# Attention scores from float32r halves in a perceiver layer: queries and keys split in two, the shift in its own product, maxima two heads at a time

## The chip, the core and the metric

The kernel runs on one core of one Trainium2 chip. The metric is the device time of one execution in microseconds, as the median of several executions. The core has five engines that work side by side and wait for each other by semaphores: TensorE (PE, matrix products into PSUM; its weight loads are listed apart as PEld), VectorE (DVE), ScalarE (ACT), GpSimd (POOL) and SyncE (SP, which here only starts DMAs). PSUM has 8 banks of 512 float32 columns on each of 128 partitions.

## The reference

One layer in float32: cross-attention from 256 queries to 4,096 keys, then a causal linear attention, then a gated feed-forward network, each behind a layer normalisation and added to x. B = 4, 16 heads of 16. The change touches the scores of the first part alone:

```python
def xattn(query, key, value):                   # query (4, 256, 256), key = value (4, 4096, 256)
    Q = query @ Wq.T + bq                       # reshaped to 16 heads of 16; K and V alike
    K = key @ Wk.T + bk
    V = value @ Wv.T + bv
    dot = einsum('bhsd,bhtd->bhst', Q, K) / sqrt(16)
    out = einsum('bhst,bhtd->bhsd', softmax(dot, axis=-1), V)
    return out @ Wh.T + bh
x = x + xattn(layernorm(x), ctx, ctx)
```

## The kernel before

**Units and steps.** A unit u is one batch with four heads; there are 16. Each head has 32 partitions of its own, of which 16 hold its dimensions, one holds the shift and the rest are zero. So a product over one head uses a quarter of PE's rows, and four heads can run at once. A unit has 16 steps (NS) of 256 keys; n counts all 256 steps.

**Two passes over the scores.** The softmax subtracts each query's exact maximum, so scores are computed twice. `maxima` (L796) makes them with 128 queries on PSUM's partitions and 512 keys on its columns (pm, L810), one bank a head, and DVE takes the maximum over the columns (mx, L817). `shift` (L821) turns the 16 maxima of a unit's queries into the negated maximum, and POOL's DMAs write it into the free row of a copy of the queries (qa, L830 and L832). As the keys have ones in that row, `scores` (L846) gets shifted scores from one product (pt, L856, keys on the partitions, 256 queries on the columns), and ACT takes the exponential of 512 columns at once (e0 to e3, L861). `product` (L866) multiplies with the values (pav, L876), where a column of ones adds the softmax's sum, and DVE adds to av (L886).

**A step's order.** The order on PE, ACT, DVE and SP is the one in which the program is written. In step n stand: scores of heads 0 and 1 together with maxima of heads 2 and 3 of the step 19 further on (LEAD = 3), then the other way round (L1122 to L1129); one half of an item that makes keys (pk, then ku on ACT) or values (pv, then v); pieces of the causal part from step 180 on (products among them from step 214); pav of step n-1. From step 237 on there are no maxima left.

**Keys.** `key` (L736) makes 512 keys for eight heads, ACT adds the bias into ku (L753), and eight DMAs on SP spread 16 rows each to kt (L756). Three kt buffers of 4,096 columns rotate over the units. They are filled with ones once, before. Queries come the same way: `project` for the first heads, `spread` for the others, with eight POOL DMAs each (L983). `finish` (L888) sends av through DRAM with twelve POOL DMAs a unit; `layernorm` and `queries` make the queries' input.

**The opening** computes all keys of the first pair of units and 19 rounds of maxima with nothing else to wait for (L1085 to L1098). After the last step, the rest of the causal part and the feed-forward network run.

**PSUM.** `bank` (L209) hands out one of eight equal banks; a new tile waits until what was last in its bank has been read.

Of the kernel before, what the change touches and what calls it, by code (L numbers as in the profile page):

```python
# [12 lines left out]
F32 = mybir.dt.float32  # L13
I32 = mybir.dt.int32
AF = mybir.ActivationFunctionType
# [5 lines left out]
P = 128  # L21
# [18 lines left out]
def perceiver_layer(  # L40
# [27 lines left out]
    wq_sb = const.tile([P, KC, NQ * P], F32, tag="wq_sb", name="wq_sb")  # L68
    bq_sb = const.tile([P, NQ], F32, tag="bq_sb", name="bq_sb")

    bk_sb, bqu_sb = (const.tile([P, KC], F32, tag=name, name=name) for name in ("bk_sb", "bqu_sb"))

    def load_queries():
# [7 lines left out]
        nc.scalar.dma_start(out=wq_sb, in_=wqP)  # L81
        nc.scalar.dma_start(out=bq_sb, in_=bqP)

# [110 lines left out]
    qT = qkT = keep.tile([P, NQ, B * T], F32, tag="qT", name="qT")  # L194
    kts = [keep.tile([P, S], F32, tag=f"kt{i}", name="kt") for i in range(3)]
    qk = [kts[1][:, t * 2 * D : (t + 1) * 2 * D] for t in range(NT)]
# [10 lines left out]
    psum = ctx.enter_context(tc.tile_pool(name="psum", bufs=8, space=PSUM))  # L207

    def bank(shape, name):  # L209

        return psum.tile(shape, F32, tag="b", name=name)
# [3 lines left out]
    def causal_in(b, norm_late=None):  # L215
# [21 lines left out]
        def queries_keys(i):  # L237
            t, zT = tiles[i], got[0]
            ps = bank([P, 2 * D], "pqk")
            for k in range(KC):  # L240
                product4(
                    ps, zT[:, k, i * P : (i + 1) * P], rest[3][:, k, : 2 * D],
                    start=k == 0, stop=k == KC - 1,
                )
            nc.vector.tensor_tensor(qk[t], ps, rest[4][:, : 2 * D], ALU.add)
            sqs[i] = lnp.tile([P, 2 * D], F32, tag="sq", name="sq")
# [42 lines left out]
    def qk_turned(t):  # L289
# [3 lines left out]
        (nc.scalar.copy if t >= NT - 2 else nc.vector.tensor_copy)(qkT[:, :, t * P : (t + 1) * P], ps)  # L293

    def feature(n, part):
        i = 2 * (n % 4) + part
        return kts[2 if n % 8 < 4 else 0][:, i * 2 * T : (i + 1) * 2 * T]

    def features(n):

        b, q = divmod(n, NQ)
        cs = slice(b * T, (b + 1) * T)
        pfs = [bank([P, 2, T], "pf") for _ in range(4)]
        for s in range(2):
            for i, pf in enumerate(pfs):
                rows = slice(32 * i, 32 * i + 32)
                nc.tensor.matmul(  # L309
                    pf[:, s, :], lhsT=rest[5][rows, q // 2, :], rhs=qkT[rows, 2 * s + q // 2, cs],  # L310
# [133 lines left out]
    def start_causal():  # L444
# [91 lines left out]
        tc, xr, load_x, load_queries, load_rest, ctxT, wq_sb, bq_sb, bqu_sb, wkP, bk_sb, wvP, eps, ident, layernorm, product4,  # L536
        qT, kts, lnp, dram, bank, rest, start_causal, wff, place, masks)
# [4 lines left out]
    masks(late.tile([P, 3, P], F32, tag="mask", name="mask"))  # L542
    att = late.tile([P, NT, D], F32, tag="att", name="att")
# [683 lines left out]
```

## Time and profile before

| what | us |
|---|---|
| median of 3 runs | 1184.56 (1184.26 to 1185.65) |
| span of the profiled execution, first to last instruction | 1182.7 |
| opening, to the first pt | 74.3 |
| steps 0 to 236 | 930.8 |
| steps 237 to 255 | about 58 |
| after the last pav | about 119 |
| PE, DVE, ACT, POOL busy | 1171.0, 904.8, 696.5, 236.8 |
| exponentials on ACT, 1,024 of them | 529.3 |
| reduces on DVE, 1,024 of them | 634.9 |

The profile was taken in an execution of its own, of which the span is known. A busy share is the time with at least one instruction running; the ends of products on PE are modelled, so a full PE is not PE at its peak. In a group's row stand line, engine, operation, what it writes and reads, shapes, the number of instructions, busy time and mean length, and the idle time before them with what ended it. In the chain, each step is what released the next, from the last instruction back. The f32 products appear twice as often as the program has them.

### The profile page before, as it was taken

The page shows a single profiled execution, that of the slowest core. Times are in us where ns is not written, and L with a number is a line of the kernel's source. Part 1 is how long each engine was busy: PE and PEld are TensorE (multiplying, and loading weights), DVE is VectorE, ACT ScalarE, POOL GpSimd, SP SyncE. Part 2 cuts the span into 40 slices and gives each one's busy share as a digit, 9 for nine tenths or more (in the row PEclk, how much of TensorE's full clock was granted, in tenths as well). Part 3 has the DMA queues.
Part 4 walks back from the last instruction along what each step waited for, and adds up shares of the span by engine and source line. Part 5 has one row for each costly group of instructions (what it writes and reads, how often), then busy time and mean ns, then how long its engine had stood idle before and what let it go on. Part 6 is the DMA issues. An engine that isn't in the chain of part 4 may idle for free.

```text
span 1182.7 us, 42980 instructions
## 1 busy us (share of the span) xinstructions
PE 1171.0 (99%) x18024; PEld 798.5 (68%) x18024; DVE 904.8 (77%) x1723; ACT 696.5 (59%) x1444; POOL 236.8 (20%) x443
## 2 busy tenths in 40 slices
PE   8999999999999999999999999999999999999998
PEld 4476667766776677667766776667666666667777
DVE  7987787777777777877777877798887788567753
ACT  4456666666666655666666665666664456876442
POOL 3730302011111212120202020303031132213210
PEclk8999999999999999999999999999999999999999
DMA  6562442234223432333224322432233112000000
GB/s 211 145 208 66 115 121 81 61 103 114 85 78 87 118 96 74 81 111 101 83 76 117 93 80 75 113 113 83 66 105 111 39 42 69 11 2 10 10 11 18
DMA packets 55160, 99.99 MB, mean 85 GB/s; under 512 B 23392, under 2 KB 28056, under 8 KB 54968
## 3 DMA queue, kind: packets, MB, share of 16 engines
q1 hardware_dynamic: 44904, 91.84, 26.2%
q0 software_dynamic: 9440, 4.81, 2.1%
q8 instruction: 143, 2.34, 0.8%
q10 hardware_dynamic: 624, 0.59, 0.2%
q14 instruction: 49, 0.40, 0.1%
HBM read 76.13 MB, written 3.21 MB: 67 GB/s over the span
## 4 chain that ended last, share of the span: by engine, by line
PE 97%; DVE 2%; ACT 1%; issue 0%; POOL 0%; ACTq 0%; POOLq 0%
PE pt L856 23%; PE pm L810 19%; PE pav L876 19%; PE pv L188 11%; PE pk L188 11%; PE pg L582 2%; PE pd L598 2%; PE pu L582 2%; PE pa L335 1%; PE pqk L188 1%; PE po L361 1%; DVE mx L817 1%; PE py L409 1%; PE pf L309 1%; PE py L188 1%; PE pa L340 1%
## 5 line engine op out<-in xcount | busy, mean ns | idle before, releaser
L861 ACT ACTIVATE e<-pt 128x512 f32<-128x512 f32 x1024 | 529.3, 602 | 374.4 <-PE pm L810 356.6
L817 DVE TENSOR_REDUCE mx<-pm 128x1 f32<-128x512 f32 x1024 | 634.9, 683 | 127.0 <-PE pm L810 126.7
L856 PE MATMUL pt<-qa,kt 32*128 32x256 f32 x4096 | 501.4, 388 | 0.7 <-DVE qa L842 0.5
L810 PE MATMUL pm<-kt,qT 32*128 32x512 f32 x2048 | 498.4, 617 | 0.1
L856 PEld LDWEIGHTS pt<-qa,kt 32*128 32x128 f32 x4096 | 318.0, 184 | 124.0 <-ACT v L781 42.4
L876 PE MATMUL pav<-e,v 128*32 128x256 f32 x4096 | 269.1, 380 | 0.0
L810 PEld LDWEIGHTS pm<-kt,qT 32*128 32x128 f32 x2048 | 181.3, 191 | 15.7 <-DVE mx L817 4.9
L876 PEld LDWEIGHTS pav<-e,v 128*32 128x32 f32 x4096 | 128.5, 110 | 74.0 <-issue 4.6
L886 DVE TENSOR_TENSOR av<-pav,av 128x256 f32<-128x256 f32 x240 | 101.6, 423 | 57.8 <-PE pav L876 57.3
L188 PE MATMUL pv<-wv_sb,wff 128*32 128x128 f32 x4096 | 137.3, 276 | 0.0
L188 PE MATMUL pk<-wff,wk_sb 128*32 128x256 f32 x2048 | 137.1, 389 | 0.0
L188 PEld LDWEIGHTS pv<-wv_sb,wff 128*32 128x32 f32 x4096 | 104.3, 109 | 43.1 <-DVE mx L817 43.1
L188 PEld LDWEIGHTS pk<-wff,wk_sb 128*32 128x32 f32 x2048 | 54.7, 110 | 66.6 <-DVE mx L817 38.8
L925 POOL TENSOR_TENSOR oT<-oT,bvT 128x64 f32<-128x64 f32 x32 | 8.6, 290 | 357.8 <-DVE oT L922 356.2
L908 POOL DMA_DIRECT2D oT<-scr x112 | 66.5, 626 | 22.1 <-DMA scr<-av 19.0
L753 ACT ACTIVATE ku<-pk,bk_sb 128x256 f32<-128x256 f32 x128 | 63.2, 495 | 12.6 <-PE pk L188 11.1
L832 POOL DMA_DIRECT2D qa<-neg x60 | 33.1, 564 | 133.8 <-DVE neg L829 96.3
L781 ACT COPY v<-pv 128x256 f32<-128x256 f32 x128 | 51.3, 401 | 9.7 <-PE pv L188 9.7
L352 DVE TENSOR_TENSOR at<-pa,mask 128x384 f32<-128x384 f32 x34 | 17.3, 551 | 19.5 <-PE pa L340 19.5
L983 POOL DMA_DIRECT2D qT<-qu x56 | 26.8, 486 | 14.6 <-ACT qu L980 11.1
L316 ACT ACTIVATE kt<-kt,shift 128x512 f32<-128x512 f32 x32 | 22.3, 727 | 8.4 <-DVE kt L315 8.4
L315 DVE TENSOR_SCALAR kt<-pf,low,top 128x512 f32<-128x512 f32 x32 | 23.7, 803 | 4.4 <-PE pf L309 4.3
(146 smaller groups left out, 645.3 us busy)
## 6 DMA issues: line engine op xcount, KB each, us to landing
wff<-in_ctxT_dram SPq DMA_DIRECT2D x128, 512.0 KB
kt<-ku SPq DMA_DIRECT2D x510, 32.0 KB
scr<-av POOLq DMA_DIRECT2D x14, 128.0 KB, 2.1
oT<-scr POOLq DMA_DIRECT2D x112, 8.0 KB, 2.7
xr<-in_x_dram SPq DMA_DIRECT2D x4, 256.0 KB
out_dram<-o SPq DMA_DIRECT2D x8, 128.0 KB
qa<-neg POOLq DMA_DIRECT2D x60, 1.0 KB, 3.5
qT<-qu POOLq DMA_DIRECT2D x56, 16.0 KB, 3.7
```

The source lines that it names most:

```text
L188: nc.tensor.matmul(out[js], lhsT=lhsT[:, js], rhs=rhs, **flags)
L582: nc.tensor.matmul(ps[:, i, :], lhsT=w[:, k, ns], rhs=zT[:, k, :], start=k == 0, stop=k == KC - 1)
L753: nc.scalar.activation(ku[:, cs], made.pop(), AF.Identity, bias=bk_sb[:, m : m + 1])
L781: nc.scalar.copy(to.rearrange("p t (h d) -> p t h d", d=HD + 1)[:, :, :, :HD], made.pop().rearrange("p t (h d) -> p t h d", d=HD),)
L810: nc.tensor.matmul(pm, lhsT=qT[rows, q, ts], rhs=kt[rows, c * CH : (c + 1) * CH], start=True, stop=True,)
L817: nc.vector.tensor_reduce(mx[:, i, j, c : c + 1], pm, AX.X, ALU.max)
L832: nc.gpsimd.dma_start(out=qa[32 * j : 32 * j + 1, :].rearrange("o (p i) -> o p i", i=2), in_=neg[:, j, :])
L856: nc.tensor.matmul(pt[:, i, :], lhsT=kt[rows, ks], rhs=qa[rows, :], start=True, stop=True)
L861: nc.scalar.activation(e, pt, AF.Exp, scale=0.25)
L876: nc.tensor.matmul(pav[32 * h : 32 * h + 32, :], lhsT=v[:, t % KT, c0 : c0 + 32], rhs=es[n, h][:, i, :], start=i == 0, stop=i == 1,)
L886: nc.vector.tensor_tensor(avs[u], pav, avs[u], ALU.add)
L908: queue.dma_start(out=oT[:, k, q % 2, j], in_=scr[32 * j : 32 * j + HD, k * P : (k + 1) * P].rearrange("e (r a) -> r e a", a=16),)
```

## The change

Queries and keys are split: hi is the value rounded to float32r, lo is what is left. A head's 32 rows hold hi and lo of its 16 dimensions in turn. The queries are stored twice, as (hi, lo) and as (lo, hi), so two float32r products in a row, `turn` 0 and 1, give hi*hi + lo*lo and hi*lo + lo*hi, accumulated in PSUM. There is no free row for the shift; it has a product of its own, with ones as weights over two rows that hold the hi and lo of the negated maximum. It opens the accumulation.

PSUM is divided: four single banks (tag b) and two pairs (tag d). A pair takes the maxima of two heads, which one DVE instruction reduces, 128x1024 to 128x2. pt, pk, pv and pav use single banks only; other tiles use halves of pairs from step 237 on, and both kinds in turn after the last step. Keys are split on POOL after ACT's bias (the first on DVE), and four DMAs a key, 64 rows each, replace eight of 16 rows. kt has one tile for each unit and 512 keys. Queries are all projected densely and split, and four SP DMAs a unit (`unit_queries`) bring them into rows. The ones in kt and POOL's copy for qa go. The shift of a unit is eight POOL DMAs in place of four.

```diff
-    psum = ctx.enter_context(tc.tile_pool(name="psum", bufs=8, space=PSUM))
-    def bank(shape, name):
-        return psum.tile(shape, F32, tag="b", name=name)
+    psum = ctx.enter_context(tc.tile_pool(name="psum", bufs=1, space=PSUM))
+    halves_left, rotation = [], itertools.cycle((False,) * 4 + (True,) * 4)
+    def double(name):
+        return psum.tile([P, 2, CH], F32, tag="d", name=name, bufs=2)
+    def bank(shape, name, single=False):
+        mode = None if single else place.get("banks")
+        if mode == "halves" or (mode == "all" and next(rotation)):
+            if not halves_left:
+                pair = double(name)
+                halves_left.extend([pair[:, 1, :], pair[:, 0, :]])
...
+        return psum.tile(shape, F32, tag="b", name=name, bufs=4)
...
+        def halved(to, x, engine):
+            hi, lo = to
+            engine.tensor_copy(hi, x)
+            engine.tensor_tensor(lo, x, hi.bitcast(F32), ALU.subtract)
...
             def out(part):
                 cs = slice(part * (CH // 2), (part + 1) * (CH // 2))
                 nc.scalar.activation(ku[:, cs], made.pop(), AF.Identity, bias=bk_sb[:, m : m + 1])
-                for h in range(8 if part == 1 else 0):
-                    r0 = 32 * (h % 4) + 1
+                if part == 0:
+                    return
+                halved((khl[:, 0], khl[:, 1]), ku, engine)
+                for u in (2 * p, 2 * p + 1):
+                    kts[u, c] = key_tile(u % 3, c, F32R)
+                for h in range(4):
+                    half, side = divmod(h, 2)
                     queues[h].dma_start(
-                        out=kts[(2 * p + h // 4) % 3][r0 : r0 + HD, c * CH : (c + 1) * CH],
-                        in_=ku[h * HD : (h + 1) * HD, :],
+                        out=kts[2 * p + half, c][side::2].bitcast(F32),
+                        in_=khl[64 * half : 64 * half + 64, side].bitcast(F32),
                     )
...
+        def unit_queries(u):
+            b, q = divmod(u, NQ)
+            qa = qas[u] = small.tile([P, 2, T], F32R, tag="qa", name="qa", bufs=3)
+            for turn in range(2):
+                for side in range(2):
+                    nc.sync.dma_start(
+                        out=qa[(side + turn) % 2 :: 2, turn].bitcast(F32),
+                        in_=qhl[64 * (q % 2) : 64 * (q % 2) + 64, side, 2 * b + q // 2, :].bitcast(F32),
+                    )
...
-            pms = [bank([P, CH], "pm") for _ in heads]
-            def products():
-                for j, pm in zip(heads, pms):
+            pm = double("pm")
+            def products(turn):
+                for k, j in enumerate(heads):
                     rows = slice(32 * j, 32 * j + 32)
                     nc.tensor.matmul(
-                        pm, lhsT=qT[rows, q, ts], rhs=kt[rows, c * CH : (c + 1) * CH],
-                        start=True, stop=True,
+                        pm[:, k], lhsT=qa[rows, turn, i::2], rhs=kt[rows, :], start=turn == 0, stop=turn == 1
                     )
             def reduce():
-                for j, pm in zip(heads, pms):
-                    nc.vector.tensor_reduce(mx[:, i, j, c : c + 1], pm, AX.X, ALU.max)
+                nc.vector.tensor_reduce(mx[:, i, heads[0] : heads[0] + 2, c], pm, AX.X, ALU.max)
...
-                nc.gpsimd.tensor_copy(qa, qT[:, q, b * T : (b + 1) * T])
+                nhl = small.tile([P, 4, 2, 2], F32R, tag="nhl", name="nhl")
+                halved((nhl[:, :, 0], nhl[:, :, 1]), neg, nc.vector)
                 for j in range(4):
-                    nc.gpsimd.dma_start(
-                        out=qa[32 * j : 32 * j + 1, :].rearrange("o (p i) -> o p i", i=2), in_=neg[:, j, :]
-                    )
+                    for side in range(2):
+                        row = 32 * j + side
+                        nc.gpsimd.dma_start(
+                            out=sh[row : row + 1, :].rearrange("o (p i) -> o p i", i=2).bitcast(F32),
+                            in_=nhl[:, j, side].bitcast(F32),
+                        )
...
+            def shifts():
+                for j, pt in zip(heads, pts):
+                    rows = slice(32 * j, 32 * j + 2)
+                    nc.tensor.matmul(
+                        pt, lhsT=ones[rows, :], rhs=sh[rows, :].unsqueeze(1).to_broadcast([2, 2, T]),
+                        start=True, stop=False,
+                    )
-            def products(i):
+            def products(i, turn):
                 for j, pt in zip(heads, pts):
                     rows = slice(32 * j, 32 * j + 32)
-                    ks = slice((2 * w + i) * P, (2 * w + i + 1) * P)
-                    nc.tensor.matmul(pt[:, i, :], lhsT=kt[rows, ks], rhs=qa[rows, :], start=True, stop=True)
+                    k0 = (2 * (w % 2) + i) * P
+                    nc.tensor.matmul(
+                        pt[:, i, :], lhsT=kt[rows, k0 : k0 + P], rhs=qa[rows, turn],
+                        start=False, stop=i == 1 and turn == 1,
+                    )
...
+            def all_maxima(g, between=None):
+                groups = [maxima(g, heads) for heads in ((0, 1), (2, 3))]
+                for turn in range(2):
+                    for products, _ in groups:
+                        products(turn)
+                for _, reduce in groups:
...
+                    reduce()
...
-                    for heads in ((0, 1), (2, 3)) if s < NU * NS else ((0, 1, 2, 3),):
-                        products, exps = scores(n, heads)
-                        more = maxima(s, [h for h in range(4) if h not in heads])
-                        products(0)
-                        more[0]()
-                        products(1)
-                        exps()
-                        more[1]()
+                    firsts = [scores(n, heads) for heads in ((0, 1), (2, 3))]
+                    if s < NU * NS:
+                        others = [maxima(s, heads) for heads in ((2, 3), (0, 1))]
+                        (shift0, first0, exps0), (shift1, first1, exps1) = firsts
+                        (most0, reduce0), (most1, reduce1) = others
+                        shift0()
+                        most0(0)
+                        first0(0, 0)
+                        most0(1)
+                        first0(0, 1)
+                        first0(1, 0)
+                        shift1()
+                        first0(1, 1)
+                        most1(0)
+                        first1(0, 0)
+                        first1(0, 1)
+                        first1(1, 0)
+                        most1(1)
+                        first1(1, 1)
+                        exps0()
+                        reduce0()
+                        exps1()
+                        reduce1()
+                    else:
+                        place["banks"] = "halves"
+                        for shifts, products, exps in firsts:
+                            shifts()
...
+                    if w == NS - 9 and u + 2 < NU:
+                        unit_queries(u + 2)
```

## The prediction

> **What bounds the kernel now.** I read the engines' shares first, then the chain that ended last, then the costliest groups, and last the timeline of one steady step. Shares, chain and groups, from the page:
>
> ```profile
> span 1182.7 us, 42980 instructions
> PE 1171.0 (99%) x18024; PEld 798.5 (68%) x18024; DVE 904.8 (77%) x1723; ACT 696.5 (59%) x1444; POOL 236.8 (20%) x443
> ...
> PE 97%; DVE 2%; ACT 1%; issue 0%; POOL 0%; ACTq 0%; POOLq 0%
> ...
> L861 ACT ACTIVATE e<-pt 128x512 f32<-128x512 f32 x1024 | 529.3, 602 | 374.4 <-PE pm L810 356.6
> L817 DVE TENSOR_REDUCE mx<-pm 128x1 f32<-128x512 f32 x1024 | 634.9, 683 | 127.0 <-PE pm L810 126.7
> L856 PE MATMUL pt<-qa,kt 32*128 32x256 f32 x4096 | 501.4, 388 | 0.7 <-DVE qa L842 0.5
> L810 PE MATMUL pm<-kt,qT 32*128 32x512 f32 x2048 | 498.4, 617 | 0.1
> ```
>
> PE carries 97% of the chain, but its busy time is modelled. The program holds 1,024 pm products and the page counts 2,048: an f32 product is two hardware instructions. One steady step, from the timeline (start, length, engine, line, operation):
>
> ```profile
> 502.99 0.48 PE L856 MATMUL pt<-qa,kt 32*128 32x256 f32 x2
> 503.00 0.71 PE L810 MATMUL pm<-kt,qT 32*128 32x512 f32 x2
> ...
> 504.17 2.48 DVE L817 TENSOR_REDUCE mx<-pm 128x1 f32<-128x512 f32 x4 [0.62 <-PE pm L810]
> ...
> 504.31 2.06 ACT L861 ACTIVATE e<-pt 128x512 f32<-128x512 f32 x4 [1.10 <-PE pm L810]
> ...
> 504.93 0.59 PEld L188 LDWEIGHTS pk<-wff,wk_sb 128*32 128x32 f32 x16 [0.33 <-DVE mx L817]
> 504.93 1.07 PE L188 MATMUL pk<-wff,wk_sb 128*32 128x256 f32 x16
> ...
> 505.82 1.05 PE L876 MATMUL pav<-e,v 128*32 128x256 f32 x16
> ...
> 506.79 0.48 PE L856 MATMUL pt<-qa,kt 32*128 32x256 f32 x2
> ```
>
> The step repeats every 3.81 us, almost without exception up to 860 us. Its loop: scores begin (506.79); the first maximum's reduce starts 1.18 later and takes 0.69; pk, which needs that reduce's bank, loads 0.07 after it; pav follows 0.89 after pk, the next scores 0.98 after pav. 1.18 + 0.69 + 0.07 + 0.89 + 0.98 = 3.81. So this one wait stands about where the score stream ends: PE is full, but not by much.
>
> **The scores in the changed step.** Read instruction by instruction, an f32 pass of 256 columns repeats on its 32 rows every 0.216 us and one of 512 every 0.43: 0.84 ns a column (granted clock 0.997). If an f32 product multiplies operands in two parts, four part products in two instructions, each instruction carries two, 0.42 ns a column each. A float32r operand has one part, so I estimate one instruction at 0.42: 0.110 us for 256 columns, 0.216 for 512. Nothing in the trace runs float32r; the other end is the f32 pass's 0.84. I take 0.42.
>
> Per 32 rows and step, before: 4 passes of 256 and 2 of 512, 2,048 columns at 0.84, 1.72 us. After: one shift of 512, four products of 256, two maxima of 512, 2,560 columns at 0.42, 1.08. 0.64 us of streaming goes. Were PE the only limit, that would be 237 steps x 0.64 = 152 us. I do not expect that, because of the banks.
>
> **The banks.** Before, eight banks serve everything. After, four single banks hold pt, pk or pv, and pav, and two pairs hold pm. The changed program's waits say who follows whom: pk or pv takes the bank of head 0's pt of the same step (it waits for exp e0), pav that of head 1, the next step's shifts of heads 0 to 2 wait for e2, e3 and the copy out of pk or pv, and the shift of head 3 waits for DVE's addition of pav. Everything on PE stands behind these waits in program order.
>
> The new loop, from the first shift's weight load: load 0.10, shift 0.216, three products at 0.110 put the fourth product of heads 0 and 1 at 0.65. But the shift of head 3 stands in front of it. The addition ends 0.56 after the scores begin (506.79 to 507.36), PE sees it 0.07 later, the weight load takes 0.10: the fourth product starts at 0.745. Stream 0.107, drain 0.16 (a pass's 0.374 less its stream of 0.213) and the 0.20 between that end and the exponential in the rows: e0 starts at 1.21, lasts 0.60, is seen by PE 0.06 later (zT to pqu showed 0.05). pk loads at 1.87; score streaming ended near 1.3, so PE stands about 0.5 us. Then 0.89 and 0.98 as before: 3.74. DVE (two reduces of 1.13, the 0.605 spacing plus 512 columns at 1.03 ns, from 0.68 for 512 columns against 0.22 for the 64 of neg<-mx; and an addition of 0.42) and ACT (four at 0.49, 0.5 for the copy) fit in with about 1 us to spare. 0.07 x 237 steps = 17 us less.
>
> **Weight loads.** Loads of 128 columns on the same rows stand 0.107 apart at the start of a step (506.792, 506.900), and a load goes under the previous product (load 506.900, that product 506.896 to 507.109, the next at 507.113). Under a 0.107 stream it just fits; I take 0.107. Lower end: the 32-column loads, about 0.03; first load and shift 3's load then save 0.08 a step, 3.66. Upper end: a whole load row of 0.185 between products, which makes the step 3.95.
>
> TensorE: Matmul & The Clock Gate (Part 3, The mechanism) speaks against the change: weight loads overlap products only of other row groups. The rows above differ for f32. By that rule the four loads of heads 0 and 1 would add 0.43 to the loop: 4.16, some 83 us more than before. The same page (Weight-path perf modes) lets 128 columns load quickly where the type is not FP32, which would be nearer 3.66; no row here shows it.
>
> **Opening** (18.3 to 73.0 us: 19 rounds of maxima). Before, eight banks keep DVE at 0.605 a reduce, 2.42 a round. After, the four products are issued first pass of both pairs, then second pass: the second pair's first pass waits for its old reduce, and the first pair's second pass stands behind it. From that reduce's end 0.07 + 0.10 + 0.22 + 0.20 = 0.6 until DVE can start. A round is 1.13 + 1.21 (the second reduce to its end) + 0.60 = 2.94, 19 of them 55.9. Before, the stretch took 54.7 with its own gaps. DVE's normalisation pieces, halving the first queries and keys and a first pm nearer 19 than 18.3 add some 3.5; the filling of kt and seven blocks of query DMAs were beside other work and give nothing. +5; ends -8 (no such wait, 19 x 2.26) and +9.
>
> **Closing steps** (19 from about 1005 us, no maxima). Four heads' shifts come first, so all products wait for shift 3: the addition (0.63 after the scores begin) puts e0 at about 1.65 and pav no earlier than 2.3: 3.28 a step without other work. Before, pt and pav alone took 2.08 (1029.43 to 1031.51) and pieces were added to that; after, a step with a long piece is some 0.4 longer, a short one up to 1.2. Over 18 steps 9; with pieces moved under the waits 8. Ends -3 (half the streaming gone, no wait) and +12.
>
> **Keys, queries, shift.** A key was eight DMAs straight from ku. Now POOL copies and subtracts first: 0.8 (twice the 0.40 of qa<-qT) and 1.04 (sq, the same shape), then four DMAs on SP. POOL's finish of a unit runs 568.6 to 577.7; every second unit one key stands behind it, and reaches kt about 15 us after its step began, when four steps of 3.74 have passed. Seven times 0 to 1 us: +1; ends 0 and 10 (each landing 1.5 late). SP has fewer issues per key (four of 0.6 for eight), so its context loads are not later; four query DMAs a unit fit there. The shift's DMAs double, 8 x 0.56 = 4.5, and land 3.5 after issue: 8.6 us after the step in which they begin, against 11.2 until needed; late would be the first shift of a unit. qa's copy on POOL goes, which nobody waited for. Head by head, copying half values costs DVE 0.3 more a unit, under its spare 1 us.
>
> **After 1062 us.** The rotation of four singles and two pairs gives the same eight banks; PE is busy 116 of 121 us there. A pair is free only when both halves are: 0, ends -1 and +4.
>
> Sum: -17 + 5 + 8 + 1 + 0 = -3, a span of 1179.7. The runs' median of 1184.56 stands 1.9 above the profiled span, which I add: 1181.6, told as 1181. A measurement tells 0.2%, about 2.4 us, from no change.
>
> **The rivals.**
> - *A shorter loop.* Short weight loads or a shift 3 that holds nothing up: 3.66, 0.15 x 237 = 35 less in place of 17: 1163. For it: the addition misses its ideal place by only 0.1. Against: f32 loads of this width were never shorter.
> - *Weight loads show* (other side). At float32r's pace each of three products waits for its load: 3.95, +0.14 x 237 = 34, with +14 elsewhere 1232. It decides once a load costs over 0.14 between products, where the loop passes 3.81.
> - *A float32r pass is no faster than an f32 pass, 0.84 ns a column.* The fourth product then starts at 1.39 with shift 3 no longer in the way: about 4.28, +0.47 x 237 = 111; opening and closing lose some 30: 1325. For it: single f32 transposes of 128 columns repeat at 0.117, 0.91 ns a column. Against: the part count above. FP8 and Floating Point Precision (TensorE Precision Notes) lists four passes for true FP32 and a truncated read otherwise, which agrees with one part product, without giving a rate.
>
> **Chances.** My sum's case 0.52: within it +-12 us, so 0.27 faster, 0.08 same, 0.17 slower. Shorter loop 0.24, faster. Loads that show 0.12, the slow pass 0.12, both slower. Faster 0.51, same 0.08, slower 0.41. The likeliest case's own range is 1169 to 1194. For 8 in 10 I go down to 1140 (a loop of 3.66 with the opening and closing at their better ends) and up to 1240 (loads that show); outside lie the case of the slow pass and a twentieth below.
>
> **What would show it.** Steady steps of 3.74; PE's idle time before pk and pv near 0.5 us with ACT e as releaser, PE busy under 90%; pm and pt products at half their spacing; e0 as the chain's link in place of mx; first pt near 79 us; closing steps of 3.3 where nothing else runs. Steps of 3.2 would show that banks do not hold PE; steps over 4 that a float32r pass or its load costs more than I took; waits of pm for kt every 32 steps, that keys are late. I am wrong above all if e0 does not gate pk.

## The result and the profile after

The changed kernel takes 1272.18 us (median, 1270.21 to 1274.76) against 1184.42 for the kernel before on the same chip: a ratio of 1.074, 95% interval 1.0725 to 1.0755. It is 7.4% slower; 1181 was forecast, with a range of 1140 to 1240. The profiled execution has a span of 1268.4 us, 85.7 more than before.

The page of the changed kernel: its span, the engines' shares, two of its strips (40 slices of the span, in tenths), and the four groups that answer to those of before.

```profile
span 1268.4 us, 44207 instructions
PE 1126.2 (89%) x19032; PEld 784.7 (62%) x19032; DVE 872.4 (69%) x1242; ACT 693.7 (55%) x1439; POOL 358.8 (28%) x571
...
PE   6889989999999999999999998999999888878888
...
PEclk8889999999999999999999999999999988789899
...
L929 ACT ACTIVATE e<-pt 128x512 f32<-128x512 f32 x1024 | 528.7, 603 | 397.9 <-PE pt L921 376.5
L868 DVE TENSOR_REDUCE mx<-pm 128x2 f32<-128x1024 f32 x512 | 601.5, 1217 | 67.5 <-PE pm L863 60.3
L863 PE MATMUL pm<-kt,qa 32*128 32x512 f32 x2048 | 346.6, 427 | 20.2 <-DVE mx L868 9.6
L921 PE MATMUL pt<-qa,kt 32*128 32x256 f32 x4096 | 318.8, 284 | 0.0
```

PE's busy share fell from 99% to 89%. The strip shows PE standing most in the first slices and in the last eight, and the clock strip falls at the same two ends. A digit of 9 hides less idle time in between. The same stretch of the main loop, before and then changed (start and end, length, busy time and instructions of PE, PEld, DVE, ACT and POOL, then granted clock, DMA share and GB/s):

```profile
180.00:900.00 720.00, 720.00 (x12064) 495.46 (x12060) 570.81 (x1056) 445.18 (x936) 126.40 (x232) 1.00 0.32 92
```

```profile
180.00:900.00 720.00, 663.53 (x13014) 474.06 (x13008) 555.18 (x714) 450.00 (x948) 235.54 (x363) 1.00 0.43 113
```

So PE is 92% busy there, in place of 100%, with the clock at 1.00 in both. The group of pt products still has 4,096 instructions, but these are now two float32r products of one instruction each, where they were one float32 product of two; their busy time fell from 501.4 to 318.8, while the shift's own products are a new group with 266.3.

The stage table is read from DVE's 256 additions of av, one a step. It is the measure for all that follows (us, from the profiled executions):

| kernel | first addition of av | next 237 steps | median step | 18 closing steps | tail | span |
|---|---|---|---|---|---|---|
| before | 81.3 | 924.4 | 3.81 | 57.7 | 119.2 | 1182.7 |
| changed | 97.2 | 918.0 | 3.74 | 91.1 | 162.2 | 1268.4 |
| difference | +15.9 | -6.5 | | +33.4 | +42.9 | +85.7 |

So the median step came out as the prediction said, to the hundredth of a microsecond, but the main loop as a whole gained 6.5 us where 16 were forecast, and the two ends that were put at +13 together cost 92. One steady step of the changed kernel, from the timeline (start, length, engine, line, operation):

```profile
524.69 0.50 PE L912 MATMUL pt<-sh,ones 2*128 2x512 f32 x2
...
524.83 0.42 DVE L954 TENSOR_TENSOR av<-pav,av 128x256 f32<-128x256 f32 x1 [0.72 <-PE pav L944]
...
525.31 0.18 PEld L912 LDWEIGHTS pt<-sh,ones 2*128 2x128 f32 x1
...
525.91 2.06 ACT L929 ACTIVATE e<-pt 128x512 f32<-128x512 f32 x4 [1.31 <-PE pt L921]
526.56 0.59 PEld L183 LDWEIGHTS pk<-wff,wk_sb 128*32 128x32 f32 x16 [0.49 <-ACT e L929]
526.56 1.07 PE L183 MATMUL pk<-wff,wk_sb 128*32 128x256 f32 x16 [0.29 <-ACT e L929]
...
527.45 1.05 PE L944 MATMUL pav<-e,v 128*32 128x256 f32 x16
...
528.42 0.50 PE L912 MATMUL pt<-sh,ones 2*128 2x512 f32 x2
```

The shift of the fourth head (weight load at 525.31) waits for the addition that ends at 525.25; e0 starts 1.22 after the scores, pk 1.87, pav 0.89 after pk, the next scores 0.97 after pav. Before pk the weight loads stand 0.49 and the products 0.29, and the releaser of both is ACT's e. The forecast had 1.21, 1.87, 0.89 and 0.98, with PE standing about 0.5.

The two ends, in stretches (columns as in the stretches above). First the changed kernel, closing steps and tail:

```profile
1010.00:1106.00 96.00, 80.79 (x890) 48.63 (x889) 35.76 (x89) 48.84 (x98) 11.42 (x25) 0.82 0.02 4
1106.00:1190.00 84.00, 63.71 (x490) 46.42 (x489) 39.17 (x89) 29.28 (x53) 16.29 (x35) 0.88 0.03 7
1190.00:1268.00 78.00, 65.46 (x402) 51.85 (x400) 30.68 (x65) 24.77 (x45) 6.97 (x16) 0.98 0.03 11
```

Then the same work in the kernel before:

```profile
1005.00:1062.00 57.00, 56.82 (x781) 36.18 (x778) 33.12 (x86) 46.36 (x95) 9.15 (x20) 1.00 0.03 7
1062.00:1182.00 120.00, 116.42 (x904) 90.29 (x899) 69.24 (x154) 53.48 (x99) 23.28 (x51) 1.00 0.04 12
```

In the tail PE stood 3.6 us before and 32.8 now, and is busy for 129.2 us with what took 116.4, at a granted clock of 0.88 and 0.98 instead of 1.00. What it waits for is told by the waits of single products (the trace names a pair by the first tile in it; in brackets the idle time and its releaser):

```profile
1024.96 0.48 PE L356 MATMUL po<-feat 64*128 64x256 f32 x1 [1.58 <-ACT avT L388]
...
1144.56 0.86 PE L382 MATMUL pu<-at,va 128*32 128x256 f32 x16 [1.29 <-DVE hT L612]
...
1128.71 3.43 PE L606 MATMUL pf<-zT,wff 128*128 128x256 f32 x8 [4.37 <-DVE feat L336]
```

None of the three needs that data. The first is a product of the causal scores (pa), placed in the second half of the pair whose first half holds po; it waits until ACT has copied po out. The second is po behind pu, whose reader is hT; the third pg behind pf, whose reader is feat. In the changed program's waits, 31 products of closing and tail wait for the reader of the other half of their own pair (24 carry the wait themselves, for 7 it stands in an instruction just ahead); in the program of before there is no such wait. The bookkeeping of tiles and their readers goes by the tile, and a pair is one tile.

### The profile page after: what moved, and what is told of

It reads as the page before. It is cut to its first block, busy times and chain, and to the rows that moved or that the text cites. A ratio compares the mean times of both kernels' runs of the same rounds, so it can differ in the third digit from the quotient of the medians.

```text
span 1268.4 us, 44207 instructions
## 1 busy us (share of the span) xinstructions
PE 1126.2 (89%) x19032; PEld 784.7 (62%) x19032; DVE 872.4 (69%) x1242; ACT 693.7 (55%) x1439; POOL 358.8 (28%) x571
## 5 line engine op out<-in xcount | busy, mean ns | idle before, releaser
L868 DVE TENSOR_REDUCE mx<-pm 128x2 f32<-128x1024 f32 x512 | 601.5, 1217 | 67.5 <-PE pm L863 60.3
L863 PE MATMUL pm<-kt,qa 32*128 32x512 f32 x2048 | 346.6, 427 | 20.2 <-DVE mx L868 9.6
L921 PE MATMUL pt<-qa,kt 32*128 32x256 f32 x4096 | 318.8, 284 | 0.0
L921 PEld LDWEIGHTS pt<-qa,kt 32*128 32x128 f32 x4096 | 307.6, 186 | 5.6
L912 PE MATMUL pt<-sh,ones 2*128 2x512 f32 x1024 | 266.3, 475 | 6.2 <-DVE av L954 3.1
L912 PEld LDWEIGHTS pt<-sh,ones 2*128 2x128 f32 x1024 | 138.5, 184 | 121.4 <-ACT v L825 45.6
L863 PEld LDWEIGHTS pm<-kt,qa 32*128 32x128 f32 x2048 | 157.9, 193 | 32.6 <-DVE mx L868 17.3
L771 POOL CAST khl<-ku 128x512 fp32r<-128x512 f32 x63 | 39.3, 624 | 294.7 <-ACT ku L792 256.4
L888 POOL DMA_DIRECT2D sh<-nhl x120 | 64.7, 554 | 77.2 <-PE pm L863 63.2
L772 POOL TENSOR_TENSOR khl<-ku,khl 128x512 fp32r<-128x512 f32 x63 | 80.5, 1278 | 5.1
L825 ACT COPY v<-pv 128x256 f32<-128x256 f32 x128 | 51.9, 405 | 17.4 <-PE pv L183 17.4
```

Source lines behind the costliest of these rows:

```text
L772: engine.tensor_tensor(lo, x, hi.bitcast(F32), ALU.subtract)
L863: nc.tensor.matmul(pm[:, k], lhsT=qa[rows, turn, i::2], rhs=kt[rows, :], start=turn == 0, stop=turn == 1)
L868: nc.vector.tensor_reduce(mx[:, i, heads[0] : heads[0] + 2, c], pm, AX.X, ALU.max)
L888: nc.gpsimd.dma_start(out=sh[row : row + 1, :].rearrange("o (p i) -> o p i", i=2).bitcast(F32), in_=nhl[:, j, side].bitcast(F32),)
L912: nc.tensor.matmul(pt, lhsT=ones[rows, :], rhs=sh[rows, :].unsqueeze(1).to_broadcast([2, 2, T]), start=True, stop=False,)
L921: nc.tensor.matmul(pt[:, i, :], lhsT=kt[rows, k0 : k0 + P], rhs=qa[rows, turn], start=False, stop=i == 1 and turn == 1,)
```

## Experiments

Theory A: the division of the banks into four single ones and two pairs costs all of the 92 us at the ends; float32r and the halves of keys and queries do not. The rivals: the lighter steps and the clock they get, the late first queries, float32r itself. The table holds every run; the differences are discussed below it.

| run | time, us | ratio to before, interval | first addition | next 237 | median step | closing | tail |
|---|---|---|---|---|---|---|---|
| tail_sep | 1213.5 | 1.0247 (1.0230 to 1.0265) | 98.0 | 917.5 | 3.74 | 78.3 | 118.8 |
| f32_pairs | 1276.5 | 1.0806 (1.0769 to 1.0843) | 100.1 | 931.5 | 3.82 | 80.9 | 162.3 |
| eight | 1110.7 | 0.9386 (0.9372 to 0.9401) | 80.8 | 852.6 | 3.40 | 55.2 | 118.8 |
| order | 1235.2 | 1.0436 (1.0421 to 1.0452) | 92.6 | 885.9 | 3.59 | 92.2 | 162.0 |
| tail_four | 1259.4 | 1.0638 (1.0617 to 1.0659) | 98.6 | 920.9 | 3.74 | 101.3 | 137.0 |
| all8 | 1195.1 | 1.0086 (1.0063 to 1.0110) | 100.8 | 919.9 | 3.74 | 54.9 | 118.8 |
| main_only | 1180.9 | 0.9971 (0.9962 to 0.9980) | 85.6 | 918.6 | 3.74 | 55.6 | 118.8 |
| eight_split | 1104.9 | 0.9324 (0.9306 to 0.9341) | 82.2 | 849.4 | 3.40 | 54.8 | 118.8 |
| eight_pm | 1112.4 | 0.9387 (0.9358 to 0.9416) | 81.3 | 856.7 | 3.40 | 54.8 | 118.8 |
| best | 1095.0 | 0.9247 (0.9233 to 0.9261) | 80.6 | 837.3 | 3.40 | 55.2 | 119.0 |

### The pairs taken away behind the main loop

```diff
-        return psum.tile([P, 2, CH], F32, tag="d", name=name, bufs=2)
+        return pairs_psum.tile([P, 2, CH], F32, tag="d", name=name)
...
         if mode == "halves" or (mode == "all" and next(rotation)):
-            if not halves_left:
-                pair = double(name)
-                halves_left.extend([pair[:, 1, :], pair[:, 0, :]])
...
+            if "more" not in place:
+                pair_pool.close()
+                place["more"] = ctx.enter_context(tc.tile_pool(name="more", bufs=4, space=PSUM))
+            return place["more"].tile(shape, F32, tag="c", name=name)
```

> Four new single banks take the place of the two pairs once the last maximum is done; everything up to there is as in the changed kernel. Theory A (the pairs cause the loss behind the main loop: a piece that writes one half of a pair waits for the reader of the piece in its other half, PE stands, and its clock falls): the stretch from the first step without maxima to the last addition of av falls from 91 us to 60 to 68, what follows it from 162 to 118 to 124, the granted clock there returns to above 0.95, and the time is about 1272 - 68 = 1204 us. Rival B (the pairs are not the cause: the clock falls on account of the lighter closing steps, or the new places of masks and attention buffers hold the pieces up): the two stretches stay at 85 to 92 and 155 to 162 us, the time at 1260 to 1272.

The tail went from 162.2 to 118.8, below the 119.2 of before, and the time fell by 59 us. The last stretch of this run:

```profile
1093.00:1212.00 119.00, 115.72 (x898) 90.04 (x890) 68.92 (x152) 53.09 (x98) 23.20 (x51) 1.00 0.04 12
```

PE stands 3.3 us and has its clock back at 1.00, behind closing steps at 0.89. So the low clock in the tail came with PE's waits there and went with them; nothing else in the tail was changed. The closing steps fell only from 91.1 to 78.3, where 60 to 68 was expected: 20.6 of their loss of 33.4 is something else.

### The division of the banks alone, with float32

The kernel before gets the changed kernel's banks and two-head reduces, and keeps its float32 scores:

```diff
-            pms = [bank([P, CH], "pm") for _ in heads]
+            pm = double("pm") if heads else None
...
-                for j, pm in zip(heads, pms):
-                    nc.vector.tensor_reduce(mx[:, i, j, c : c + 1], pm, AX.X, ALU.max)
+                if heads:
+                    nc.vector.tensor_reduce(mx[:, i, heads[0] : heads[0] + 2, c], pm, AX.X, ALU.max)
```

> The kernel before with its float32 scores, its query copy and its shift, and of the change only the division of the banks (four single ones, two pairs, the closing pieces in halves of pairs) and the maxima of two heads at a time. Theory A: the closing steps and the tail lose most of what they lost in the changed kernel, 50 to 76 us, with no float32r in the program; the opening loses 5 to 10 by rounds of 2.9 us in place of 2.4; e0 starts about 1.3 us behind the first score product, so a step is 1.3 + 0.6 + 0.07 + 0.89 + 0.98 = 3.85 us, +0.04 x 237 = 9. Time about 1184 + 65 + 8 + 9 = 1266 us. Rival B (the loss behind the main loop comes from float32r, the keys' halves, or the lighter steps and the clock they get): closing and tail stay within 10 us of the kernel before, time about 1205 us.

The tail takes 162.3 us with not one float32r product in the program, the opening 18.8 more than before and the closing steps 23.2 more. The division, with the two-head reduces that it brings, makes the kernel before 8% slower. Of the changed kernel's 92 us at the ends it shows 85: the closing steps lose 23.2 here and 33.4 there, where four shifts stand first in a step as well. The main loop lost 7 us (9 expected, by a step of 3.85; the median is 3.82).

### Four banks for the end of the kernel

```diff
-        mode = None if single else place.get("banks")
-        if mode == "halves" or (mode == "all" and next(rotation)):
...
         return psum.tile(shape, F32, tag="b", name=name, bufs=4)
```

> The changed kernel, but from the end of the maxima on the two pairs stay empty: closing steps and tail have only the four single banks in rotation. No half of a pair is shared, and there are half as many banks. Theory A1 (the loss behind the main loop is the shared pair: one half waits for the other half's reader): the tail, 162 us in the changed kernel and 119 with eight separate banks, is shorter than 162 although four banks are gone: 125 to 150. Theory A2 (the loss is the number of tiles that may be open at once, whatever is shared): the tail is as long as in the changed kernel or longer, 162 to 200. The closing steps, whose four scores and pieces now share four banks, do not tell: 85 to 110 us against 91.

With the pairs left empty and half the banks gone, the tail is 25 us shorter than with all eight of which four are in pairs: 137.0 against 162.2. Sharing a pair does harm beyond the lack of a bank. The closing steps took 101.3, longer than in the changed kernel: there four banks for scores and pieces are too few.

### One rotation over eight banks behind the maxima

```diff
+        if place.get("banks") and "more" not in place:
+            pair_pool.close()
+            place["more"] = ctx.enter_context(tc.tile_pool(name="more", bufs=4, space=PSUM))
+        if "more" in place and next(rotation):
+            return place["more"].tile(shape, F32, tag="c", name=name)
         return psum.tile(shape, F32, tag="b", name=name, bufs=4)
```

> As the run with four new single banks behind the maxima, but all eight banks now serve scores, products and pieces in one rotation, where there the scores kept the old four and the pieces had the new four. If the 20 us that the closing steps still lost there (78.3 us against 57.7 before the change) came from the division into four and four, they fall to 55 to 60, as with eight banks throughout (55.2), the tail stays at 119, and the span is 1212.6 - 22 = 1191 us. If it came from the four shifts that stand first in a closing step, they stay at 75 to 80 and the span at 1210.

Closing steps of 54.9 us, shorter than before the change, with the four shifts still first in each: the rest of their loss was the split into four banks for scores and four for pieces. The wait of the fourth shift for the addition goes with it: the five light steps take 1.21 to 2.49 here and 3.16 to 3.23 in the changed kernel. The span, 1194.4, is 3 above the expected one because the opening came out at 100.8. The opening's code is the same in the changed kernel, tail_sep, tail_four and this run, which gave 97.2, 98.0, 98.6 and 100.8: so much it varies.

### Pairs in the main loop alone

```diff
+        pools, shares = ((8,), (4, 2), (8,))[len(stages)], ExitStack()
...
+            if len(stages) == 2:
+                pm = double("pm")
+            else:
+                pms = [bank([P, CH], "pm") for _ in heads]
```

> Pairs in the main loop alone: the opening has eight single banks and reduces of one head, the main loop the changed kernel's four single banks and two pairs, closing steps and tail eight single banks. If the division of the banks is what the opening lost by, the first addition of av comes at 80 to 83 us (97.2 in the changed kernel, 80.8 with eight banks throughout); if the late first queries and keys (first maximum at 21.9 in place of 18.3 us) are, at 94 to 97. Main loop 918, closing 56, tail 119. Span 81 + 918 + 56 + 119 = 1174 us, or 1190.

The first addition comes at 85.6 with the first maximum no earlier (22.5 us): 11.6 of the opening's 15.9 us are the banks, give or take the 3.6 by which openings vary. The expectation of 80 to 83 was missed behind the first pt at 76.5: from there to the first addition it is 9.1 us, against 6.6 in the changed kernel. ACT loads its table for the exponential (1.28 us) only after the first scores, at 77.56, where the changed kernel does so before them, at 90.06 with the first pt at 90.58; and from 79 to 86 us the granted clock is 0.76, against 1.00 from 93 to 98 us there. Why the load stands later was not tested. What is left of the change is 1180.9 us, 0.3% faster than before.

How the pairs cost the opening is read in a stretch of it. The changed kernel, then the kernel with eight single banks (same columns):

```profile
25.00:45.00 20.00, 16.26 (x172) 7.20 (x168) 13.04 (x14) 5.90 (x13) 7.83 (x10) 0.84 0.62 179
```

```profile
25.00:45.00 20.00, 19.19 (x229) 9.11 (x219) 17.59 (x34) 7.81 (x18) 9.75 (x14) 0.98 0.74 210
```

Two pairs hold one round of maxima and no more. While PE makes keys or queries between two rounds, DVE has nothing left to reduce (13.0 of 20 us busy against 17.6), and while DVE reduces, PE stands (16.3 against 19.2) and its clock goes to 0.84. With eight banks both run ahead of each other.

### Two changes of order in the changed kernel

```diff
-                        shift1()
                         first0(1, 1)
+                        shift1()
...
-                for turn in range(2):
-                    for products, _ in groups:
+                for products, _ in groups:
+                    for turn in range(2):
                         products(turn)
```

> Two changes of order on PE in the changed kernel, in two stages that can be read apart. In a main step the fourth product of heads 0 and 1 goes ahead of the shift of heads 2 and 3, which waits for DVE's addition of av: e0 then starts 0.095 us earlier, a step is 3.64 in place of 3.735, 22 us less over 237 steps. If e0 is not what pk and so the step wait for, steps stay at 3.73. In the opening both passes of a pair go together, the first pair's ahead of the second's: a round falls from 2.98 to 2.46 us (two reduces of 1.23 back to back), 19 rounds, 10 us less, if the first pair's second pass behind the second pair's reduce is what each round stands for; otherwise the first pt stays near 90.5 us. Closing and tail stay at 91 and 162. Time about 1240 us.

The step fell to 3.59, more than the 3.64 expected. From this kernel's timeline, the first score product, e0 and the weight loads of pv in one step:

```profile
539.77 0.50 PE L912 MATMUL pt<-sh,ones 2*128 2x512 f32 x2
...
540.84 2.07 ACT L929 ACTIVATE e<-pt 128x512 f32<-128x512 f32 x4 [1.26 <-PE pt L921]
541.49 0.81 PEld L183 LDWEIGHTS pv<-wv_sb,wff 128*32 128x32 f32 x32 [0.34 <-ACT e L929]
```

e0 starts 1.07 after the scores in place of 1.22, and the loop is shorter by these 0.15. So e0 sets the step through pk's or pv's bank, and in the changed kernel it was held up by a shift that does not concern its own head. The opening gained 4.6 us, not 10; rounds stand 2.55 apart where they run back to back (27.41, 29.96, 32.50 for two reduces each), but with a piece between two rounds DVE still waits up to 3.5. With openings that vary by 3.6, only the sign is sure.

### Eight single banks throughout, with float32r

```diff
-            pm = double("pm")
+            pms = [bank([P, CH], "pm") for _ in heads]
...
-                nc.vector.tensor_reduce(mx[:, i, heads[0] : heads[0] + 2, c], pm, AX.X, ALU.max)
+                for pm, j in zip(pms, heads):
+                    nc.vector.tensor_reduce(mx[:, i, j, c : c + 1], pm, AX.X, ALU.max)
...
-        return psum.tile(shape, F32, tag="b", name=name, bufs=4)
+        return psum.tile(shape, F32, tag="b", name=name, bufs=8)
```

The tiles of the maxima and of the scores also come from the rotation in turn, one pair of heads after the other.

> The changed kernel with eight single banks, as before the change, and the maxima of one head at a time in four reduces; float32r, halves of keys and queries and the shift's own pass stay. The division of the banks is thereby taken out everywhere. If e0 and the addition of av set the step only through the four single banks, pk now waits for the first reduce: it starts about 0.95 us behind the scores and takes 0.61; 0.95 + 0.61 + 0.07 + 0.89 + 0.98 = 3.5 us a step (237 x 0.235 = 56 less); opening rounds 2.45 in place of 2.98 (10 less); closing and tail within 8 us of the kernel before (about 68 less). Time about 1272 - 56 - 10 - 68 = 1138 us, 4% under the kernel before. If float32r's passes or weight loads themselves set the step, it stays at 3.7 and the time is about 1195 us.

1110.7 us, 6.1% faster than before and 12.7% faster than the changed kernel. Opening (80.8), closing (55.2) and tail (118.8) are all slightly better than before the change, although the first maximum still starts at 21.7 us in place of 18.3. The step is 3.40. Its loop in the timeline of this run:

```profile
604.20 0.50 PE L904 MATMUL pt<-sh,ones 2*128 2x512 f32 x2
...
604.98 2.48 DVE L860 TENSOR_REDUCE mx<-pm 128x1 f32<-128x512 f32 x4 [0.22 <-PE pm L854]
...
605.72 0.59 PEld L183 LDWEIGHTS pk<-wff,wk_sb 128*32 128x32 f32 x16 [0.28 <-DVE mx L860]
...
606.61 1.05 PE L936 MATMUL pav<-e,v 128*32 128x256 f32 x16
...
607.59 0.51 PE L904 MATMUL pt<-sh,ones 2*128 2x512 f32 x2
```

pk again takes the bank of the first reduce, as before the change: 0.78 + 0.68 + 0.06 + 0.89 + 0.98 = 3.39. A reduce of one head is done 0.68 after it starts, one of two heads 1.22, and e0, which starts 1.09 after the scores, ends at 1.69. The single reduces cost DVE 0.03 us more a head (2.48 for four against 2.36 for two pairs) and bring the first bank back soonest.

### The first reduce earlier

```diff
                         shift0()
                         most0(0)
+                        most0(1)
                         first0(0, 0)
-                        most0(1)
...
+                        first0(1, 1)
                         shift1()
-                        first0(1, 1)
```

> The kernel with eight single banks, where the loop of a step is: first reduce 0.78 us behind the scores, 0.69 long, 0.06 until pk, 0.89, 0.975 = 3.40. On PE both passes of the maxima of heads 2 and 3 now go ahead of the products of heads 0 and 1, which wait in PE's queue for their shift to stream (second pass at 0.355 behind the first one in place of 0.23), and the shift of heads 2 and 3 goes behind the fourth product of heads 0 and 1. If pk waits for the first reduce, the reduce and the loop come 0.125 us earlier: 3.275 us a step, 237 x 0.125 = 30 us less, 1081. If it waits for e0, as in the changed kernel, e0 comes about 0.05 to 0.1 later by the maxima ahead of it, and steps are 3.40 or longer.

A miss: the step stayed at 3.40. The first pass of the maxima starts at 593.39, the second at 593.74, the reduce at 594.16; without the edit it was 600.81, 601.16 and 601.59. The second pass comes 0.35 after the first wherever it stands in the queue, so it had not been waiting for the products named in the expectation. What sets the 0.35 is not shown.

### The long steps of every second unit

With eight banks the fourth step of every second unit takes 7.3, 4.4, 4.6, 7.4, 3.4 and 7.6 us (in the changed kernel 5.2, 3.7, 4.6, 3.8, 4.2 and 7.5). PE waits there for kt. Two runs move the ten reads that `finish` puts on a queue:

```diff
-            for k in range(KC):
+            def read(k):
...
-                        for at, piece in zip((8, 9, 10, 12), left):
+                        for at, piece in zip((3, 5, 8, 9, 10, 12), left):
```

> The kernel with eight single banks, and of finish(u) only the two DMAs that write av are issued on POOL's queue at the unit's first step; the ten that read it back, which stood there for 3.7 us of waiting and 5.8 of issuing ahead of the next key's halves, are issued five at a time two and four steps later. If the fourth step of every second unit is long (7.3, 4.4, 4.6, 7.4, 3.4, 7.6 us against 3.4) because that key is late, it falls to 3.4 to 3.6, and the time from 1110.7 to 1110.7 - 14 = 1097 us. If the key is late for another reason (its own cast and subtraction, 1.9 us, and four DMAs on SP, 3.1 us), these steps stay and the time is 1108 to 1112.

A gain of 5.8 us instead of 14; the fourth steps took 5.4, 3.4, 4.7, 5.1, 3.4 and 7.4. POOL's timeline says why:

```profile
134.62 0.67 POOL L961 DMA_DIRECT2D sums<-av  x1
139.69 2.37 POOL L969 DMA_DIRECT2D oT<-scr  x4 [4.40 <-DMA scr<-av]
142.02 0.62 POOL L973 DMA_DIRECT2D dn<-sums  x1
142.60 1.22 POOL L969 DMA_DIRECT2D oT<-scr  x2
143.75 0.69 POOL L762 CAST khl<-ku 128x512 fp32r<-128x512 f32 x1
```

The reads were written behind the key's cast and stand in front of it. The other engines keep the order of the program, POOL is scheduled, and the scheduler drew the reads forward, where POOL stands 4.4 us for the data and the cast behind it. The last run puts them on SP's queue and keeps the order of the run before it:

```diff
-                    queue.dma_start(
+                    nc.sync.dma_start(
...
-                        for at, piece in zip((3, 5, 8, 9, 10, 12), left):
+                        for at, piece in zip((2, 4, 8, 9, 10, 12), left):
```

> The same with the ten reads of av issued on SP's queue, which keeps the order of the program, five two steps and five four steps behind the unit's end (on POOL the order of the program was not kept: they stood ahead of the key's cast even when written behind it). If the long fourth steps of every second unit (14 us together with eight banks, 9 with the reads written later on POOL) come from keys that stand behind these reads on POOL, they go to about the normal step: 10 to 14 us less than the run beside it, about 1069. If they come from the key's own 1.9 us of cast and subtraction and its four DMAs, which now stand behind the reads on SP, nothing is gained or steps get longer: 1081 or more.

The fourth steps are 3.39 to 3.40 in all six units; 17.4 us less than the run beside it, whose six steps had 17.2 over 3.40 together; 10 to 14 were expected. Two strips of its page:

```profile
PE   6999999999999999999999999999999999999998
...
PEclk8999999999999999999999999999999999999999
```

1095.0 us is 7.5% less than the kernel before.

## Why the prediction was wrong

**The step that failed** is the shortest one: "The rotation of four singles and two pairs gives the same eight banks", priced at 0 with ends of -1 and +4. It cost 42.9. It counted banks and asked when a pair comes free ("only when both halves are"), which is about the next tile in it. The loss is inside a pair that is held: the second half's product waits for the first half's reader (31 such waits), PE stands, and what PE then does runs at a lower clock: 29 us more standing and 13 more busy. tail_sep shows it undone, f32_pairs shows it without the rest of the change.

**Closing steps**, +8 with an upper end of 12: measured +33.4. The mechanism named (all products wait for shift 3) is there: five light steps take 3.16 to 3.23 against 3.28 forecast, and lose 5.2 us together. Mis-sized were the other thirteen, most of them with long pieces, which lose 28.2. What was missed is that the pieces had shared pairs (12.8, by tail_sep) and that scores and pieces no longer borrowed from each other's banks (23.4 more, by all8; the wait for shift 3 is part of this), after which the closing steps are 2.8 shorter than before the change.

**Opening**, +5 with an upper end of 9: measured +15.9. The round itself was right (2.94 forecast, 2.97 between 28.06 and 31.03 on DVE). Mis-sized was what lies between rounds: keys, queries and values were taken as covered, as they were with eight banks. They now come between the rounds, for DVE idles while PE makes them. main_only gives 11.6 of it back, eight all. The late first maximum, taken as +0.7 and measured at +3.7, cost nothing once the banks were there.

**The main loop** was right in each term of a step: float32r products 0.110 to 0.118 us apart for 256 columns and 0.22 to 0.23 for 512 (0.110 and 0.216 taken), e0 at 1.22 (1.21), pk at 1.87, a step of 3.74. The median step gives 237 x 0.075 = 18 us, as forecast; 6.5 were left in the stage. The rest of it went into late keys, 6.5 us over six units where +1 was taken and 10 was the upper end, and some 5 in the steps that carry other work. "PE busy under 90%" came out at 89% through the ends alone; the main loop has 92%.

**The rivals.** Weight loads that show, with 3.95 a step, are excluded: loads of the same 32 rows went under running products at 0.11 apart. The rule of the Trainium skill that spoke against the change (TensorE: Matmul & The Clock Gate, Part 3, The mechanism: its list says that a load overlaps only products of another row group, though its text names a background weight buffer besides) would have given 4.16 a step; the trace shows 3.74, so it does not hold for these products. A float32r pass as slow as a float32 pass is excluded by the same rows. Two readings in that rival's text were off: 1.39 is where the fourth product's stream would end (its sum of 4.28 goes by the start, 1.18), and the transposes of before repeat at 0.109 in most places, 0.85 ns a column, where 0.117 was told. A shorter loop did not come by itself: the shift stood in the way just as written, and the run with the order changed gives 3.59. The time fell outside all the cases because each took the ends of the kernel as known.

The run main_only, which has the change without its banks at the ends, measures 1180.9, next to the forecast's 1181. That is luck: its main loop gains 5.9 where 16 were forecast, and its closing steps lose nothing (2.1 less than before) where +8 was, a price that counted on the banks.

## What to carry to other kernels

A bank is worth what the waits of its tile allow: two tiles put in halves of one larger tile wait for each other's readers, and eight banks in such a form did worse than four in the tail here (162 against 137 us). When a change regroups a shared resource, price every stage that draws on it, not only the one the change is for; here each of the three stages outside the main loop lost more than the main loop gained. And a faster product is worth what its consumer can free: half the product time brought 2% of a step behind four shared banks and 11% behind eight.

## What was not expected of the hardware

- A float32r product of 256 columns repeats every 0.11 us on its rows, one of 512 every 0.22: half of one float32 pass (0.216 and 0.43), and a float32 product has two of these. Its 128-column weight load is hidden behind a product of 0.11 us on the same rows.
- The granted clock is lower in stretches where PE has gaps: 0.82 over closing steps in which PE is busy for 81 of 96 us, 0.88 at 64 of 84, 0.84 in the opening at 16 of 20, and 1.00 over the tail's work at 97% busy. The busy share alone does not set it: the end of the tail has 0.98 at 65 of 78 us, the same 84% as the closing steps, and the main loop 1.00 at 92%. These are means: in narrow windows of the changed kernel it is 0.50 (1013.2 to 1019.8 us, 1074.6 to 1088.1) or 1.00 (1020 to 1026.6). What makes it change over is not shown. A product of the feed-forward part (8 products, pg) takes 3.43 to 3.78 us in such a stretch and 2.00 elsewhere in the same tail. A sentence of the Trainium skill (Perfetto Trace Analysis, Matmul Optimizations) points the same way: the engine scales its power with its use, so products should run back to back.
- POOL's 128x512 cast to float32r takes 0.62 us and the subtraction 1.28: 1.9 for a key, where 1.84 was estimated from other shapes. What made keys late was not this but the queue in which they stand: the last run keeps both and has no long fourth step up to unit 11.
